# A graph attention layer: x_l rows of one tile in 22 pairs fetched one by one from SyncE, and the states cleared tile by tile

## Chip, cores and metric

The kernel runs on one core of a Trainium2 chip. The metric is the device time of one execution in microseconds. Before the change the median of 3 runs is 3961.25 us (3960.65 to 3964.16). The profile is of one further execution.

## The reference

A GATv2 layer with a feed-forward part, on 12,500 nodes with 128 features and 400,000 edges, sorted by their destination. `h` is the normalised and rectified input.

```python
x_l = (ln(h) @ W_l).reshape(n, H, C)          # H = 8 heads, C = 16
x_r = (ln(h) @ W_r).reshape(n, H, C)
e = (edge_attr @ W_e).reshape(-1, H, C)       # 32 attributes per edge, and a loop per node
m = leaky_relu(x_l[src] + x_r[dst] + e, 0.2)
alpha = einsum('ehc,hc->eh', m, att)
a = softmax of alpha over the edges of one destination
out = segment_sum(x_l[src] * a, dst) + bias
h = h + out
return x + h + gelu(ln(h) @ W1 + b1) @ W2 + b2
```

The costly part is `x_l[src]`: 400,000 rows in an order that only the data know.

## The kernel before

The nodes are 98 tiles of 128. First comes a **start** (`tile_gnn`): in rounds of 4 tiles, x is normalised, multiplied by W_l and written to `xl_dram` as rows of 136 words (544 bytes; 128 features and 8 ones). The x_l rows of a round are made by VectorE (L595) in one of three buffers and stored by SyncE (L603). In round 14 of the start SyncE loads the source indices of all edges (`src_sb`, L797). Meanwhile GpSimd gathers raw rows of x for 29 chosen pairs of units (L301), whose x_l rows are made later, so that these pairs need no gather of x_l.

Then comes the **edge loop** (`window_edges`). A unit is 256 edges, a pair is two units, so 512 edges in 4 tiles of 128; there are 782 pairs. The order of all engines is written out by hand (`manual_schedule`): round r runs the stages of different pairs, each with its lateness against the pair:

- `gather` (4 rounds ahead): GpSimd issues one indirect DMA (L980) per tile of 128 edges, four for a pair, into one of 12 buffers `xs`. Pairs of the 29 read their rows by one SyncE load (L975).
- `windows` (3 rounds ahead, every fourth pair): SyncE loads the edge attributes `ea` (L994), the destinations `dl` and `du` (L999, L1004), reads an address from `win_sb` into a register (L955) and loads the x_r rows `zw` (L1010).
- `place`: VectorE makes the selection matrices from `dl` (L1020) and `du` (L1027).
- `combine`: TensorE transposes the four tiles of `xs` into `z` (L1034) and adds x_r and e with one more matmul (L1037). It is the first to read the gathered rows.
- `apart`, `slope`, `bend`, `score`, `lowest`, `weigh` (L1043 to L1075): the leaky ReLU, the scores, their least value and the exponentials.
- `turn`, `keep_turned`, `collect` (L1083 to L1097): the weights are transposed, and `collect`, 6 rounds late, multiplies them with `xs` into `acc`. It is the last to read the gathered rows.
- `own_heads` (L1106, L1112) brings `acc` into a record `rec` of 16 destinations for each unit, and `put` (7 rounds late, L1122) writes both records from SyncE to `state_dram`, at an address read from `base_sb` every fourth pair. A put waits for the put before it, since the address is only known at run time.

State rows that no put writes must hold zeros and a large least score. `clear` (L745) writes those, for 7 tiles of nodes at a time and each of the two states apart: group 0 at the end of the start, then one group in every 8th round up to round 104. From round 197 on, groups of 4 node tiles whose edges are done are finished (`f_...`): their states are read back (L1173), merged, and run through the feed-forward part. In the first 196 rounds SyncE also loads all edge attributes for their mean (`ea_s`, L1129), every second round.

All loads and stores named here go through SyncE's queue in the order of the program; each waits for its semaphores there, and what follows waits behind it. In a round that order is: early steps of the finishing groups, the stages (of which SyncE has L975), `ea_s`, the clear, the finishing groups, the x_r and late x_l work, `windows`, `put`.

Of the kernel before, what the change touches and what calls it, by code (L numbers as in the profile page):

```python
# [13 lines left out]
F32 = mybir.dt.float32  # L14
BF16 = mybir.dt.bfloat16
I32 = mybir.dt.int32
U8 = mybir.dt.uint8
# [5 lines left out]
P = 128  # L23
# [19 lines left out]
OW = 172  # L43
OS = 176
PW = OR * OS
BEFORE = 12
AFTER = 3
WN = P - DE
# [14 lines left out]
BUSY = 5  # L63
LEAD = 2
KEPT = 7
BIG = 2.0**126
CAP = 2.0**120

# [76 lines left out]
def tile_gnn(  # L145
# [56 lines left out]
    src_sb = keep.tile([P, NCH * K], I32, name="src_sb")  # L202
    base_sb = keep.tile([1, NU // UP], I32, name="base_sb")
    win_sb = keep.tile([1, NU // QU], I32, name="win_sb")
    flag = keep.tile([1, 1], I32, name="flag")
    quads = [(t, min(GN, NT - t)) for t in range(0, NT, GN)]
    VAR = 6
# [532 lines left out]

    empty = keep.tile([P, H, SH], F32, name="empty")

    def clear(g):
        for st in state:
            nc.sync.dma_start(  # L745
                st.rearrange("(t p h) f -> p t (h f)", p=P, h=H)[:, g * GT : (g + 1) * GT, :],
                empty.rearrange("p h f -> p (h f)")[:, None, :].to_broadcast([P, GT, SW]),
            )

    node_stages = (  # L750
        (0, x_stats),
# [16 lines left out]
    with tc.manual_schedule():  # L768
        load_first()
        make_identity(nc, ident)  # L770
        for t in xls:
            nc.vector.memset(t[:, :, P:], 1.0)
        load_weights()
        load_x(0, min(GN, NT))
        load_raw()
        load_x(GN, min(3 * GN, NT - GN))
        for t in range(4 * GN, NT, 14):
            load_x(t, min(14, NT - t))
        load_dst()
        load_consts()  # L780
        nc.vector.memset(empty, 0.0)
        nc.vector.memset(empty[:, :, C + 1 : SH], CAP)
        rows_at = [i * 5 // 4 for i in range(len(raw))]
        for r in range(max(max(len(qs), 9) + LAST + 1, 16 + PARTS, rows_at[-1] + KEPT + 1)):
            if r == 0:
                count_up()
            for d, at in zip(raw, rows_at):
                if r == at:
                    raw_gather(d)
                if r == at + KEPT:  # L790
                    raw_store(d)
            if r == 3:
                weights()
            if r == 9:
                last_of_units()
            if r == 14:
                nc.sync.dma_start(src_sb, src)  # L797
# [24 lines left out]
        clear(0)  # L822
    pre.close()

    fast = nc.values_load(flag[0:1, 0:1], min_val=0, max_val=1)
    with tc.If(fast == 1) as cmp:
        window_edges(
            tc, n_edges, ea_t, NT, NE, NUE, ident, wer, weh, negrep, diag, nid, farw, bias_r, b2_r, w1_sb, w2_sb,
            cols, xl_dram, xl_t, xr_dram, xr_t, dc_dram, du_dram, late_dram, state_dram, state, clear, xr_steps, qs, raw_steps, raw, x_t, out_t, h_sb, src_sb, base_sb, win_sb, wid,
        )  # L830
    with cmp.Else():
        any_edges(
# [64 lines left out]

def window_edges(
    tc, n_edges, ea_t, NT, NE, NUE, ident, wer, weh, negrep, diag, nid, farw, bias_r, b2_r, w1_sb, w2_sb,
    cols, xl_dram, xl_t, xr_dram, xr_t, dc_dram, du_dram, late_dram, state_dram, state, clear, xr_steps, qs, raw_steps, raw, x_t, out_t, h_sb, src_sb, base_sb, win_sb, wid,  # L900
):


# [25 lines left out]
    with ExitStack() as es:  # L929
# [34 lines left out]
        def states_at(at):  # L964
# [4 lines left out]
                "u (n f) -> n u f", f=SH * 4  # L969
            )  # L970

        def gather(c):
            xs = rows.tile([P, KP, XW], F32, name="xs")
            if c in of_raw:
                nc.sync.dma_start(xs, late_dram[of_raw[c]["i"]])  # L975
                pairs[c]["xs"] = xs
                return
            for t in tiles_of(c):
                for j in t:
                    nc.gpsimd.indirect_dma_start(  # L980
                        out=xs[:, j, :],
                        out_offset=None,
                        in_=xl_dram,
                        in_offset=bass.IndirectOffsetOnAxis(ap=src_sb[:, c * KP + j : c * KP + j + 1], axis=0),
                    )
            pairs[c]["xs"] = xs
# [42 lines left out]
        def combine(c):  # L1029

            d, e = pairs[c], sum(edges_of(c))
            z = ps2.tile([P, EPR], F32, name="z")
            for j in range(e // P):
                nc.tensor.matmul(  # L1034
                    z[:, j * P : (j + 1) * P], d["xs"][:, j, 0:P], ident, start=(j == 0), stop=False, is_transpose=True
                )
            nc.tensor.matmul(z[:, :e], d["zw"], d["ea"][:, :e], start=False, stop=True)  # L1037
            d["z"] = z
# [51 lines left out]
        def collect(c):  # L1090
# [4 lines left out]
            for i, js in enumerate(tiles_of(c)):  # L1095
                for j in js:
                    nc.tensor.matmul(  # L1097
                        d["acc"][:, i, :], d["pt"][:, j * P : (j + 1) * P], d["xs"][:, j, :],
                        start=(j == js[0]), stop=(j == js[-1]),
                    )  # L1100

# [456 lines left out]
        CLEAR = 8  # L1558
# [379 lines left out]
```

## Time and profile before

| | |
|---|---|
| median of 3 runs | 3961.25 us |
| the profiled execution | 3956.45 us |
| its span | 3954.7 us |
| PE (TensorE) busy | 3447.8 us, 87% |
| POOL (GpSimd) busy | 2956.0 us, 75% |
| DVE (VectorE) busy | 2792.9 us, 71% |
| ACT (ScalarE) busy | 2168.7 us, 55% |
| TensorE clock granted, mean | 0.943 |

The span runs from the first to the last instruction that the profiler saw; the execution has 1.75 us around it. SP is SyncE; instructions that only issue DMAs, set registers or wait are not counted as busy, so SP has no busy time of its own, but its issues and waits can be listed. A group of instructions is shown as line, engine, operation and tiles, with its count, its busy time, the mean of one in ns, and the idle time of its engine just before it with what ended most of it. "issue" there is time in which the engine waited for nothing that the profile shows. Rows of the kind "min/median/max" give durations in ns. A row of a waits view gives the total, the count and the longest. In rows that cut the span into stretches, each engine's busy time is followed by the granted clock, the mean busy share of the 16 DMA engines and their GB/s.

### The profile page before, as it was taken

To read this page: it belongs to the slowest core of one execution; us is meant where nothing else is said; L and a number is where in the kernel's file an instruction comes from. 1 tells how busy PE (TensorE), PEld (TensorE's weight loads), DVE (VectorE), ACT (ScalarE), POOL (GpSimd) and SP (SyncE) were. 2 spreads that over 40 slices of the span, in tenths; PEclk is the share of its full clock that TensorE was granted. 3 is DMA by queue.
4 is the path that set the end of the run, shared out by engine and by line. 5 is a ranking of instruction groups with operands and counts; after the bars stand their busy time and mean duration, and the time that the engine had idled before them with its cause. 6 is when DMAs were issued, how large, how long until landed. Compare 5 with 4: busy or idle time off the path is not lost. (4 is left out here: it accounts for less than half of the span.)

```text
span 3954.7 us, 58500 instructions
## 1 busy us (share of the span) xinstructions
PE 3447.8 (87%) x18462; PEld 2358.8 (60%) x18463; DVE 2792.9 (71%) x6137; ACT 2168.7 (55%) x4747; POOL 2956.0 (75%) x3138
## 2 busy tenths in 40 slices
PE   4589898989898899999898898998889899889898
PEld 3356565656565666666665665666666566556565
DVE  6577777878776767677767776777767667667665
ACT  7445555655565555555555555555555555455444
POOL 7777777777777777777777777777777777777774
PEclk6799999999999999999999999999999999999999
DMA  8777787777666666666566666556556665655553
GB/s 225 214 183 190 195 201 194 184 176 168 164 128 124 128 122 123 128 123 120 115 122 128 124 123 128 123 119 125 117 124 125 127 122 108 122 119 114 122 118 74
DMA packets 579318, 552.09 MB, mean 140 GB/s; under 512 B 286689, under 2 KB 457282, under 8 KB 578578
## 3 DMA queue, kind: packets, MB, share of 16 engines
q1 hardware_dynamic: 478280, 330.80, 35.9%
q0 software_dynamic: 100000, 217.32, 28.5%
q8 instruction: 150, 2.46, 0.3%
q14 instruction: 168, 1.38, 0.1%
q10 hardware_dynamic: 720, 0.13, 0.0%
HBM read 482.05 MB, written 65.88 MB: 139 GB/s over the span
## 5 line engine op out<-in xcount | busy, mean ns | idle before, releaser
L980 POOL DMA_INDIRECT xs<-xl_dram,src_sb x3009 | 2841.7, 944 | 917.1 <-issue 798.0
L1075 ACT ACTIVATE p<-ab,rec 128x256 f32<-128x256 f32 x1563 | 655.2, 471 | 1025.8 <-DVE rec L1064 1021.3
L1106 DVE TENSOR_TENSOR own<-acc,diag 128x272 f32<-128x272 f32 x782 | 341.4, 437 | 811.5 <-PE acc L1097 809.5
L1097 PE MATMUL acc<-xs,pt 128*128 128x136 f32 x6250 | 891.6, 288 | 0.3 <-DVE own L1106 0.3
L1034 PE MATMUL z<-ident,xs 128*128 128x128 f32 x3125 | 552.9, 283 | 374.0 <-DMA xs<-xl_dram,src_sb 324.9
L1037 PE MATMUL z<-ea,zw 128*128 128x512 f32 x1564 | 852.7, 628 | 26.5 <-DVE ea L1020 11.3
L1034 PEld LDWEIGHTS z<-ident,xs 128*128 128x128 f32 x3125 | 398.4, 143 | 768.4 <-DMA xs<-xl_dram,src_sb 413.6
L1097 PEld LDWEIGHTS acc<-xs,pt 128*128 128x128 f32 x6250 | 820.7, 199 | 0.5 <-DVE own L1106 0.5
L1058 PE MATMUL ab<-m,negrep 128*128 128x512 f32 x1564 | 806.4, 597 | 0.0
L1088 ACT COPY pt<-pt_ps 128x512 f32<-128x512 f32 x782 | 454.9, 582 | 570.9 <-PE pt_ps L1083 568.9
L1053 DVE TENSOR_TENSOR m<-z,zs 128x512 f32<-128x512 f32 x782 | 532.8, 681 | 139.2 <-ACT zs L1048 138.1
L1083 PEld LDWEIGHTS pt_ps<-ident,p 128*128 128x128 f32 x3125 | 415.9, 148 | 360.1 <-issue 286.4
L1020 DVE TENSOR_SCALAR ea<-dl,wid 96x516 f32<-96x516 bf16 x782 | 575.8, 736 | 36.1 <-DMA dl<-dc_dram 36.1
L1064 DVE TENSOR_REDUCE rec<-ab 128x2 f32<-128x512 f32 x781 | 538.0, 689 | 13.1 <-PE ab L1058 12.5
L1083 PE MATMUL pt_ps<-ident,p 128*128 128x128 f32 x3125 | 499.4, 285 | 1.2 <-ACT xr L627 0.9
L1048 ACT ACTIVATE zs<-z 128x512 f32<-128x512 f32 x782 | 472.7, 604 | 41.7 <-DMA xs<-xl_dram,src_sb 34.9
L1112 DVE TENSOR_REDUCE rec<-own 128x34 f32<-128x272 f32 x782 | 340.8, 436 | 26.7
L1043 PE MATMUL ab<-ne,farw 128*128 128x512 bf16 x782 | 313.0, 400 | 28.4 <-ACT p L1075 25.7
L1037 PEld LDWEIGHTS z<-ea,zw 128*128 128x128 f32 x1564 | 256.5, 205 | 30.1 <-DVE ne L1027 10.3
L1058 PEld LDWEIGHTS ab<-m,negrep 128*128 128x128 f32 x1564 | 245.1, 194 | 1.1 <-DMA ea_s<-in_ea_t 0.7
L1043 PEld LDWEIGHTS <-farw 128*128 128x128 bf16 x782 | 79.5, 102 | 221.9 <-issue 110.2
L1075 ACT ACT_TABLE_LOAD x104 | 133.4, 1283 | 1.8
(237 smaller groups left out, 2167.4 us busy)
## 6 DMA issues: line engine op xcount, KB each, us to landing
dl<-dc_dram SPq DMA_DIRECT2D x196, 396.0 KB
ea<-in_ea_t SPq DMA_DIRECT2D x196, 256.0 KB
ea_s<-in_ea_t SPq DMA_DIRECT2D x98, 512.0 KB
xs<-xl_dram,src_sb POOLq DMA_INDIRECT x3009
state<-empty SPq DMA_DIRECT2D x28, 504.0 KB
state<-rec SPq DMA_DIRECT2D x781, 18.0 KB
f_st<-state SPq DMA_DIRECT2D x46, 288.0 KB
du<-du_dram SPq DMA_DIRECT2D x196, 64.0 KB
```

What stands on the lines that cost most here:

```text
L980: nc.gpsimd.indirect_dma_start(out=xs[:, j, :], out_offset=None, in_=xl_dram, in_offset=bass.IndirectOffsetOnAxis(ap=src_sb[:, c * KP + j ...
L1020: nc.vector.tensor_scalar(d["ea"][0:WN].rearrange("p (a b) -> p a b", b=OW), d["dl"][0:WN].rearrange("p (a b) -> p a b", b=OS)[:, :, 0:OW] ...
L1034: nc.tensor.matmul(z[:, j * P : (j + 1) * P], d["xs"][:, j, 0:P], ident, start=(j == 0), stop=False, is_transpose=True)
L1037: nc.tensor.matmul(z[:, :e], d["zw"], d["ea"][:, :e], start=False, stop=True)
L1048: nc.scalar.activation(d["zs"][:, :e], d["z"][:, :e], AF.Copy, scale=SLOPE)
L1053: nc.vector.tensor_tensor(d["m"][:, :e], d["z"][:, :e], d["zs"][:, :e], op=OP.max)
L1058: nc.tensor.matmul(d["ab"][:, :e], negrep.rearrange("p n h -> p (n h)"), d["m"][:, :e], start=False, stop=True)
L1064: nc.vector.tensor_reduce(d["rec"][:, :, CX], d["ab"].rearrange("p (u e) -> p u e", e=U), AX.X, OP.min)
L1075: nc.scalar.activation(d["p"][:, us], d["ab"][:, us], AF.Exp, bias=d["rec"][:, i, CX:SH], scale=-1.0)
L1083: nc.tensor.transpose(d["pt_ps"][:, js], d["p"][:, js], ident)
L1088: nc.scalar.copy(d["pt"][:, :e], d["pt_ps"][:, :e])
L1097: nc.tensor.matmul(d["acc"][:, i, :], d["pt"][:, j * P : (j + 1) * P], d["xs"][:, j, :], start=(j == js[0]), stop=(j == js[-1]),)
```

## The change

Of 35 pairs (31, 53, ... 779, none of the 29) GpSimd gathers only three tiles. The 128 rows of the fourth are fetched by SyncE, one DMA of 544 bytes each, into a tile of their own (`hand`, two buffers), spread over 22 rounds, 5 or 6 a round, at the start of the round. The last are issued 3 rounds before the pair's own. The byte addresses come from a small tile `hand_sb`, loaded in the start right behind `src_sb` as 35 x 128 single words and multiplied by 544 by VectorE two rounds later; SyncE reads 16 of them at a time into registers. Each row counts on one of 7 semaphores kept for this, and SyncE waits once for each tile for the full count, one round before the pair's. `combine` and `collect` read the fourth tile from `hand`.

`clear` now writes one tile of nodes in both states with one DMA: four of them at the end of the start, then one in every 4th round up to round 372, as the last thing of the round, behind the put.

```diff
+HAND_EVERY = 22
+HAND_FIRST = 31
+HAND_LEAD = 2
+HAND_READ = 16
+LANDED = 7
+CLEARED = 4
+CLEAR = 4
...
+def hand_pairs(nt, n_edges):
+    late = {c for c, _ in raw_pairs(nt, n_edges)}
+    hands = range(HAND_FIRST, n_edges // (UP * U), HAND_EVERY)
+    assert not late & set(hands)
+    return hands
...
-    def clear(g):
-        for st in state:
-            nc.sync.dma_start(
-                st.rearrange("(t p h) f -> p t (h f)", p=P, h=H)[:, g * GT : (g + 1) * GT, :],
-                empty.rearrange("p h f -> p (h f)")[:, None, :].to_broadcast([P, GT, SW]),
-            )
+    def clear(t):
+        both = state_dram[0 : UP * SR].rearrange("(a n) f -> a n f", a=UP)
+        nc.sync.dma_start(
+            both[:, (BEFORE + t * P) * H : (BEFORE + (t + 1) * P) * H].rearrange("a (p h) f -> p a (h f)", h=H),
+            empty.rearrange("p h f -> p (h f)")[:, None, :].to_broadcast([P, UP, SW]),
+        )
...
             if r == 14:
                 nc.sync.dma_start(src_sb, src)
+                nc.sync.dma_start(
+                    hand_sb,
+                    bass.AP(
+                        tensor=src.tensor, offset=src.offset + (hands[0] + 1) * UP * KU - 1,
+                        ap=[[hands.step * UP * KU, len(hands)], [NCH * K, P]],
+                    ),
+                )
+            if r == 16:
+                nc.vector.tensor_scalar(hand_sb, hand_sb, float(XW * 4), None, op0=OP.mult)
...
-        clear(0)
+        for t in range(CLEARED):
+            clear(t)
...
+        by_hand = {c: {"i": i} for i, c in enumerate(hands)}
+        landed = [tc.alloc_semaphore(f"landed{i}") for i in range(LANDED)]
+        def hand(r):
+            i, k = divmod(r + HAND_LEAD + hands.step - hands[0], hands.step)
+            if k == HAND_LEAD - 1 and 0 < i <= len(hands):
+                all_here = nc.sync.wait_ge(landed[(i - 1) % LANDED], ((i - 1) // LANDED + 1) * P * 16)
+                tc.declare_fence(all_here.ins, group=f"hand{i - 1}")
+            if not 0 <= i < len(hands):
+                return
+            d = by_hand[hands[i]]
+            if k == 0:
+                d["x"] = once.tile([P, XW], F32, name=f"hand{i % 2}")
+            for e in range(P * k // hands.step, P * (k + 1) // hands.step):
+                if e % HAND_READ == 0:
+                    d["at"] = words(hand_sb[i : i + 1, e : min(e + HAND_READ, P)], (NT * P - 1) * XW * 4)
+                row = nc.sync.dma_start(
+                    d["x"][e : e + 1, :].bitcast(U8), rows_at(xl_dram, d["at"][e % HAND_READ], 1, XW * 4)
+                )
+                row.then_inc(landed[i % LANDED], 16)
+                tc.no_tile_sem_insts.add(row.ins.name)
+                tc.add_to_no_dep_group(f"hand{i}", row.ins)
+        def row_of(c, j):
+            return by_hand[c]["x"] if c in by_hand and j == KP - 1 else pairs[c]["xs"][:, j, :]
...
                 for j in t:
+                    if c in by_hand and j == KP - 1:
+                        continue
                     nc.gpsimd.indirect_dma_start(
...
             for r in range(-AHEAD, max(last_round, groups[-1]["round"] + 18)):
                 in_round(r, early, groups[:-2])
+                hand(r)
...
-                if r > 0 and r % CLEAR == 0 and r // CLEAR < NT // GT:
-                    clear(r // CLEAR)
...
+                t, off = divmod(r, CLEAR)
+                if off == 0 and CLEARED <= t + CLEARED < NT and t >= 0:
+                    clear(t + CLEARED)
```

More of the change, by code (lines that the diff above doesn't have):

```diff
@@ L204, in tile_gnn @@
     win_sb = keep.tile([1, NU // QU], I32, name="win_sb")
+    hands = hand_pairs(NT, n_edges)
+    hand_sb = keep.tile([len(hands), P], I32, name="hand_sb")
     flag = keep.tile([1, 1], I32, name="flag")
@@ L828, in tile_gnn @@
             tc, n_edges, ea_t, NT, NE, NUE, ident, wer, weh, negrep, diag, nid, farw, bias_r, b2_r, w1_sb, w2_sb,
-            cols, xl_dram, xl_t, xr_dram, xr_t, dc_dram, du_dram, late_dram, state_dram, state, clear, xr_steps, qs, raw_steps, raw, x_t, out_t, h_sb, src_sb, base_sb, win_sb, wid,
+            cols, xl_dram, xl_t, xr_dram, xr_t, dc_dram, du_dram, late_dram, state_dram, state, clear, xr_steps, qs, raw_steps, raw, x_t, out_t, h_sb, src_sb, base_sb, win_sb, hand_sb, hands, wid,
         )
@@ L899, in window_edges @@
     tc, n_edges, ea_t, NT, NE, NUE, ident, wer, weh, negrep, diag, nid, farw, bias_r, b2_r, w1_sb, w2_sb,
-    cols, xl_dram, xl_t, xr_dram, xr_t, dc_dram, du_dram, late_dram, state_dram, state, clear, xr_steps, qs, raw_steps, raw, x_t, out_t, h_sb, src_sb, base_sb, win_sb, wid,
+    cols, xl_dram, xl_t, xr_dram, xr_t, dc_dram, du_dram, late_dram, state_dram, state, clear, xr_steps, qs, raw_steps, raw, x_t, out_t, h_sb, src_sb, base_sb, win_sb, hand_sb, hands, wid,
 ):
@@ L1034, in combine @@
                 nc.tensor.matmul(
-                    z[:, j * P : (j + 1) * P], d["xs"][:, j, 0:P], ident, start=(j == 0), stop=False, is_transpose=True
+                    z[:, j * P : (j + 1) * P], row_of(c, j)[:, 0:P], ident, start=(j == 0), stop=False, is_transpose=True
                 )
@@ L1097, in collect @@
                     nc.tensor.matmul(
-                        d["acc"][:, i, :], d["pt"][:, j * P : (j + 1) * P], d["xs"][:, j, :],
+                        d["acc"][:, i, :], d["pt"][:, j * P : (j + 1) * P], row_of(c, j),
                         start=(j == js[0]), stop=(j == js[-1]),
```

1 line of the change is left out of this document (removed).

## Prediction

> **What bounds the kernel now.** I read the page first, then the rows of the gather line, then the waits, then the chain of waits. Busy shares alone point to PE:
>
> ```profile
> span 3954.7 us, 58500 instructions
> PE 3447.8 (87%) x18462; PEld 2358.8 (60%) x18463; DVE 2792.9 (71%) x6137; ACT 2168.7 (55%) x4747; POOL 2956.0 (75%) x3138
> POOL 7777777777777777777777777777777777777774
> DMA  8777787777666666666566666556556665655553
> ```
>
> But POOL's digit never moves, although DMA falls from 8 to 5. The group and its waits say why:
>
> ```profile
> L980 POOL DMA_INDIRECT xs<-xl_dram,src_sb x3009 | 2841.7, 944 | 917.1 <-issue 798.0
> ...
> L980 POOL DMA_INDIRECT xs<-xl_dram,src_sb x3009: 940/944/1080, 151.6 to 3909.2; - x189
> ...
> POOL xs L980 <- issue: 798.0, 2618, 0.3
> PE z L1034 <- DMA xs<-xl_dram,src_sb: 324.9, 247, 4.1
> ```
>
> POOL spends 944 ns on a gather and 917.1/3009 = 305 ns before the next; no idle piece is over 0.3 us. From 151.6 to 3910.1 us that is 3009 x 1.249 = 3758 us, the whole stretch: POOL waits for nobody. PE does wait, 324.9 us in all, for gathers to land, so PE has some 8% of room. By stage, the pace is the same where the DMA engines are busiest (0.77) and where they are not (0.60):
>
> ```profile
> 200.00:1080.00 880.00, 773.39 (x4118) 525.24 (x4119) 670.11 (x1307) 473.13 (x1042) 665.14 (x705) 0.95 0.77 184
> 1980.00:3880.00 1900.00, 1703.56 (x9211) 1164.22 (x9210) 1318.73 (x2767) 1030.69 (x2109) 1436.62 (x1521) 0.96 0.60 121
> ```
>
> 665.14/880 and 1436.62/1900 are both 75.6% of POOL. The chain of waits at the end starts from the last gathers and needs about 45 us more, of PE, the last puts and the feed-forward:
>
> ```profile
> 3905.43 0.94 POOL xs L980
> ...
> 3907.92 3.38 DMA xs<-xl_dram,src_sb
> ```
>
> So the time is POOL's queue plus that tail. There are 782 pairs (29 of them fetched without POOL), so a round of the loop is 3758/782 = 4.805 us and 22 rounds are 105.7 us.
>
> **What the change removes.** `hand_pairs` gives 31, 53, ... 779: 35 pairs, each with one gather less. 35 x 1.249 = **-43.7 us** on the queue that sets the end, which leaves 104.5 us for 22 rounds. For PE nothing changes: the same 8 matmuls read `hand` in place of `xs`. PE's 8% of room covers a pace 1.2% quicker. The tail stays.
>
> **What it adds on SP.** 35 x 128 = 4480 one-row DMAs and 35 x 8 = 280 register loads of 16 words, spread over the 22 rounds before each use (about 6 rows a round). What SP has free decides. Its present load comes from its own waits:
>
> ```profile
> SPq L1122 <- DMA state<-rec: 352.9, 140, 8.2
> ...
> SPq L1122 <- DVE f_mn L1238: 0.2, 1, 0.2
> ```
>
> These are the first and the last of the 26 rows between 1980 and 2980 us; all 26 sum to 691.3 us, so SP works 308.7 of 1000 us, which is 32.6 us in 22 rounds. In 200 to 1080 us its 31 rows sum to 567.3 of 880, that is 37.6 us in 22 rounds; less the old clears (26 at 0.49 us), 36 us.
>
> No one-row DMA with a register address is in the trace. The nearest issues on SP are:
>
> ```profile
> L328 SPq DMA_DIRECT2D dc<-in_dst x1: 223/223/223, 27.9 to 27.9; - x1
> ...
> L337 SPq DMA_DIRECT2D dc<-in_dst x1: 272/272/272, 28.5 to 28.5; - x1
> ...
> L1010 SPq MOVE zw<-xr_dram x196: 29/35/42, 159.5 to 3897.5; - x196
> L1010 SPq DMA_DIRECT2D zw<-xr_dram x196: 332/343/359, 159.6 to 3897.6; - x196
> ...
> L955 SPq TENSOR_LOAD <-win_sb x196: 527/748/812, 158.7 to 3896.8; - x196
> L955 SPq TENSOR_LOAD <-base_sb x196: 299/307/331, 182.6 to 3926.9; - x196
> ```
>
> The first two fill one partition (257 and 4096 words) from fixed addresses. The third writes 96 partitions from a register address, after a move. Between two SP instructions lie some 0.045 us:
>
> ```profile
> 1510.11 0.41 SPq L994 DMA_DIRECT2D ea<-in_ea_t  x1
> 1510.57 0.42 SPq L999 DMA_DIRECT2D dl<-dc_dram  x1
> 1511.04 0.59 SPq L1004 DMA_DIRECT2D du<-du_dram  x1
> 1512.55 0.35 SPq L1010 DMA_DIRECT2D zw<-xr_dram  x1
> ```
>
> A row thus costs between 0.223 + 0.03 + 0.09 = 0.34 us and 0.343 + 0.035 + 0.09 = 0.47 us. I take **0.37**, from the middle of the two one-partition rows, whose shape it has. 128 x 0.37 = 47.4 us. A register load: 0.35 to 0.84 us with its gap; taken near the upper row, as it too follows DMA issues: 8 loads, 6 us.
>
> **The clears** move as well: 98 of 144 KB instead of 28 of 504 KB (14.1 MB both ways), one every 4 rounds up to round 376 rather than two every 8 up to 104, and now directly behind a put, on the same tensor. A clear has waited for a put before:
>
> ```profile
> SPq L745 <- DMA state<-rec: 19.6, 12, 2.2
> ...
> SPq L1122 <- DMA state<-empty: 85.8, 14, 9.3
> L745 SPq DMA_DIRECT2D state<-empty x28: 377/488/687, 153.4 to 665.0; - x28
> ```
>
> That is 1.63 us each with another issue in between; now next to nothing lies in between, so about 1.7 us of standing plus 0.45 of issue, 5.5 times in 22 rounds: 12 us of SP. The 85.8 us that puts stood behind clears shrink, but they are off POOL's path and earn nothing.
>
> From round 197 the finishing groups read the states back, and SP stands for landings that no row can fill:
>
> ```profile
> SPq L1122 <- DMA f_st<-state: 64.5, 24, 4.4
> SPq L1173 <- DMA state<-rec: 58.3, 25, 5.1
> ```
>
> 122.8 us over 585 rounds, 4.6 us in 22. SP in 22 rounds, against POOL's 104.5 us: rounds 7 to 196 (`ea_s` still loading) 36 + 47.4 + 6 + 12 = **101.4**; rounds 197 to 376 32.6 + 4.6 + 47.4 + 6 + 12 = **102.6**; later **90.6**. So SP just fits. Waits that stay, for the previous put's landing, are filled by the rows. I add 2.5 us for moments when SP is late: what stands behind it then are the window loads (L994 to L1010) that DVE's L1020 and PE's L1037 need two rounds on, and POOL feels that only after the 12 gather buffers are full, about 5 rounds (24 us) of lag.
>
> The new wait (one per hand tile) comes two rounds, 9.5 us, after the last row's issue, and a put lands within 2 us near the end:
>
> ```profile
> 3928.27 2.02 DMA state<-rec
> ```
>
> So it is normally past. Behind it in SP's queue stand the next rows, the windows and the put.
>
> On the DMA engines a row moves 544 bytes. The 72-byte packets of the puts took 7.8% of 16 engines in a 6.1 us stretch for 688 packets, 11 ns each, so even 16 pieces a row (71,680) are about 50 us per engine over 3,700: hidden.
>
> ```profile
> DMA packets 688, 0.05 MB, mean 8 GB/s; under 512 B 688, under 2 KB 688, under 8 KB 688
> ...
> q1 hardware_dynamic: 688, 0.05, 7.8%
> ```
>
> [...]
>
> **What it adds at the start.** The list of rows (`hand_sb`, 35 x 128 single words) is loaded behind `src_sb`, and DVE multiplies it two rounds later, in order:
>
> ```profile
> 71.97 0.70 SPq L797 DMA_DIRECT2D src_sb<-in_src  x1
> 76.74 1.09 DVE L595 SCALAR_TENSOR_TENSOR xl<-lr,roots_sb,bl_r 128x128 f32<-128x128 f32 x4
> ...
> 136.65 0.37 SPq L603 DMA_DIRECT2D xl_dram<-xl  x1
> ...
> 151.60 0.94 POOL L980 DMA_INDIRECT xs<-xl_dram,src_sb  x1 [0.30 <-issue]
> ```
>
> The load ahead of it:
>
> ```profile
> src_sb<-in_src SPq DMA_DIRECT2D x1, 1568.0 KB
> ...
> 72.00:74.00 2.00, 0.50 1.02 301
> ```
>
> DVE reaches the multiply at about 77.8 us. `src_sb`, 1568 KB at about 301 GB/s shared with the stores, is in by about 79. Single words were loaded before, 2 x 784 of them (L266):
>
> ```profile
> q1 hardware_dynamic: 794, 0.04, 168.2%
> ```
>
> 794 packets in the microsecond from 47 to 48, on 16 engines: 20 ns each per engine. [...] POOL loses 0 to 4 us; more if words come slower than those. I take **+4**, the upper end, as the stores queued behind the words land late too. [...] No row here shows a DMA of 35 rows.
>
> **The sum.** -43.7 + 4 + 2.5 = -37.2 us. The profiled execution took 3956.45 us (span 3954.7 and 1.75 around it): 3919.3. The median of the runs is 4.8 us above it, so **3924**; own range 3914 to 3941.
>
> **Rivals.**
> 1. **SP becomes the bound** (slower). With c the cost of a row, the first half fits only while some 54.6 + 128c stays under 104.5, c under 0.39 us. At `zw`'s 0.468 it needs 114.5 us: 8.8 us more than now in each of the 16.8 periods to round 376, +148, less 24 in the buffers; later 103, so the 18.4 periods of the second half still gain 22; with the start +4: +106, about **4067**. It is slower than before from c = 0.42 (16.8 x 2.5 = 24 + 22 - 4). For it: the wait sums, and that the row address sits in a register; against it: the one-partition issues. With also a dearer register load it goes beyond 4100.
> 2. **Marginal SP**: c near 0.41; the first half loses what the second gains: 3953 to 3969.
> [...]
> 4. **It does nothing**: PE takes over as the bound. Its 324.9 us of waiting for gathers speak against; time about 3960.
>
> **Chances.** Forecast 0.50, rival 1 0.26, rival 2 0.10, rival 3 0.11, rival 4 0.03 (rivals 2 and 4 make up "same"). A run tells about 0.2% (8 us) from no change. Faster 0.61, same 0.13, slower 0.26. Range 3908 to 4012: it takes in a row at 0.34 us (no stalls, no loss at the start: 3917), less 9 us for the spread between runs and what an overlap could add, and the lower half of rival 1; about 0.15 lies above it.
>
> **What would show it.** Right: 2974 gathers, still 944 ns with 305 between, the last one about 37 us earlier, PE's waits for gathers a little shorter, SP's row DMAs at 0.25 to 0.3 us. Wrong: POOL idle pieces of whole microseconds on the gather line (rival 1), window loads as releasers of DVE L1020; a first gather much later than 151.6 (rival 3).

## The result, and the profile after

The changed kernel takes a median of **4144.7 us** in 4 runs (4142.03 to 4151.94), against 3960.95 us (3958.65 to 3964.16) for the kernel before beside it: a ratio of 1.0466, 95% interval 1.0448 to 1.0484. It is 184 us slower, where 37 us less were forecast; the time lies above the range too (3908 to 4012). The line numbers from here on are those of the changed kernel: the gather is L1037, the place matrices L1077, `collect` L1154, the put L1179, the clear L762, the rows L1016, the register reads L982.

The page's head, and GpSimd's group on the page and in the rows of its line (shortest, median and longest in ns, first and last start):

```profile
span 4143.5 us, 67817 instructions
PE 3499.8 (84%) x18461; PEld 2394.4 (58%) x18463; DVE 2804.6 (68%) x6138; ACT 2161.9 (52%) x4747; POOL 2922.4 (71%) x3103
...
POOL 7776666656666667676667777777777777777774
...
L1037 POOL DMA_INDIRECT xs<-xl_dram,src_sb x2974 | 2808.1, 944 | 1135.4 <-issue 775.8
```

```profile
L1037 POOL DMA_INDIRECT xs<-xl_dram,src_sb x2974: 938/944/1073, 151.8 to 4094.0; - x199
```

The gathers are as forecast: 2974 of 944 ns, the first at 151.8 us (151.6 before). But POOL's digit, 7 in all 39 full slices before, is now 6 or 5 in many, up to about 2200 us, and idle time that is not "issue" has gone from 917.1 - 798.0 = 119 us to 1135.4 - 775.8 = 360 us. A view by stretch (busy time of PE, PEld, DVE, ACT and POOL, clock, DMA share, GB/s) says where:

```profile
300.00:1100.00 800.00, 635.51 (x3188) 433.41 (x3188) 525.53 (x1013) 364.79 (x806) 511.78 (x543) 0.88 0.66 151
1200.00:2150.00 950.00, 811.77 (x4294) 557.28 (x4294) 626.06 (x1323) 482.43 (x1003) 651.97 (x691) 0.92 0.59 123
2300.00:4000.00 1700.00, 1537.57 (x8374) 1050.22 (x8373) 1209.59 (x2536) 948.84 (x1944) 1285.24 (x1361) 0.97 0.62 123
```

The last stretch still has the old pace, 1285.24/1700 = 75.6% of POOL. The first has 64.0% and the second 68.6%. At 75.6% their 511.78 and 651.97 us of gathers would have taken 677 and 862 us: 123 and 88 us are lost there. The clears are issued from 153.6 to 2165.2 us; the loss ends with them.

What POOL waits for, and what stands behind that, among the waits of all engines (total, times, longest):

```profile
POOL xs L1037 <- issue: 775.8, 2543, 0.6
DVE ea L1077 <- DMA dl<-dc_dram: 332.2, 81, 9.4
POOL xs L1037 <- PE acc L1154: 256.2, 113, 9.0
PE z L1094 <- DMA zw<-xr_dram: 98.7, 28, 6.8
```

GpSimd stands 256.2 us for `acc`, so for gather buffers to come free; VectorE stands 332.2 us for `dl`, 36.1 before. `dl` comes from SyncE. One such place, SyncE's queue first, then VectorE and GpSimd in the same microseconds:

```profile
713.54 0.40 SPq L1179 DMA_DIRECT2D state<-rec  x1
718.24 0.39 SPq L762 DMA_DIRECT2D state<-empty  x1
718.73 1.93 SPq L1016 DMA_DIRECT2D hand<-xl_dram  x6
720.70 0.34 SPq L1051 DMA_DIRECT2D ea<-in_ea_t  x1
721.10 0.42 SPq L1056 DMA_DIRECT2D dl<-dc_dram  x1
```

```profile
726.22 0.75 DVE L1077 TENSOR_SCALAR ea<-dl,wid 96x516 f32<-96x516 bf16 x1 [6.44 <-DMA dl<-dc_dram]
...
731.41 0.94 POOL L1037 DMA_INDIRECT xs<-xl_dram,src_sb  x1 [2.88 <-PE acc L1154]
```

After the put's issue (713.54 to 713.94) SyncE stands 4.3 us until the put has landed and the clear may go; rows and windows wait behind. VectorE stands 6.44 us for `dl`, TensorE behind it, and GpSimd then finds no free buffer for 2.88 us. SyncE's own waits over the whole span, after and then before:

```profile
SPq L1179 <- DMA state<-rec: 269.1, 223, 4.2
SPq L762 <- DMA state<-rec: 256.5, 92, 5.3
SPq L1179 <- DVE rec L1169: 81.8, 92, 6.9
```

```profile
SPq L1122 <- DMA state<-rec: 1359.2, 547, 8.2
SPq L1122 <- DVE rec L1112: 739.1, 425, 8.9
```

Before, a put waited 739.1 us in all for its record: SyncE was ahead of the other engines and idle. After, that is 81.8 us, 63.4 of it after 2150 us: up to 1100 us SyncE hardly ever waits for work, as the next rows show (23.7 of 800 us, all that is not a put or a clear waiting for a landing). The stands of a put for the put before it have shrunk too, from 1359.2 to 269.1 us: most of that time is now filled with rows. The 256.5 us of clears standing for puts are new (21.2 before).

### The profile page after: what moved, and what is told of

Its sections match the earlier page's. It is cut to its first block, busy times and chain, and to the rows that moved or that the text cites. A ratio compares the mean times of both kernels' runs of the same rounds, so it can differ in the third digit from the quotient of the medians.

```text
span 4143.5 us, 67817 instructions
## 1 busy us (share of the span) xinstructions
PE 3499.8 (84%) x18461; PEld 2394.4 (58%) x18463; DVE 2804.6 (68%) x6138; ACT 2161.9 (52%) x4747; POOL 2922.4 (71%) x3103
## 3 DMA queue, kind: packets, MB, share of 16 engines
q0 software_dynamic: 98880, 214.89, 29.2%
## 4 chain that ended last, share of the span: by engine, by line
PE 38%; DMA 24%; DVE 10%; POOL 9%; issue 8%; SPq 8%; ACT 4%; POOLq 0%; DVEq 0%; ACTq 0%
POOL xs L1037 9%; PE acc L1154 9%; DMA xs<-xl_dram,src_sb 9%; PE z L1094 9%; PE ab L1115 7%; DMA state<-rec 5%; PE pt_ps L1140 5%; PE z L1091 4%; SPq L1016 3%; DMA dl<-dc_dram 2%; PE ab L1100 2%; DMA du<-du_dram 2%; DVE rec L1121 2%; SPq L982 2%; DMA zw<-xr_dram 1%
## 5 line engine op out<-in xcount | busy, mean ns | idle before, releaser
L1037 POOL DMA_INDIRECT xs<-xl_dram,src_sb x2974 | 2808.1, 944 | 1135.4 <-issue 775.8
L1094 PE MATMUL z<-ea,zw 128*128 128x512 f32 x1564 | 873.3, 642 | 187.2 <-DMA zw<-xr_dram 98.7
L1154 PE MATMUL acc<-xs,pt 128*128 128x136 f32 x6180 | 901.7, 292 | 4.1 <-DVE own L1163 3.5
L1154 PEld LDWEIGHTS acc<-xs,pt 128*128 128x128 f32 x6180 | 830.1, 203 | 5.2 <-DVE own L1163 4.1
L1115 PE MATMUL ab<-m,negrep 128*128 128x512 f32 x1564 | 816.0, 604 | 0.2 <-issue 0.2
L1077 DVE TENSOR_SCALAR ea<-dl,wid 96x516 f32<-96x516 bf16 x782 | 576.4, 737 | 332.3 <-DMA dl<-dc_dram 332.2
L1091 PE MATMUL z<-ident,xs 128*128 128x128 f32 x3090 | 523.7, 281 | 257.4 <-DMA xs<-xl_dram,src_sb 155.2
L1140 PE MATMUL pt_ps<-ident,p 128*128 128x128 f32 x3125 | 508.1, 289 | 8.3 <-ACT xr L644 4.6
L1105 ACT ACTIVATE zs<-z 128x512 f32<-128x512 f32 x782 | 473.5, 606 | 36.1 <-DMA state<-empty 28.3
L1100 PE MATMUL ab<-ne,farw 128*128 128x512 bf16 (+1 forms) x781 | 316.2, 405 | 44.9 <-ACT p L1132 41.6
L1192 DVE TENSOR_REDUCE part<-ea_s 128x1 f32<-128x1024 f32 x98 | 118.8, 1212 | 37.6 <-DMA ea_s<-in_ea_t 37.0
```

What stands on the lines that cost most here:

```text
L1037: nc.gpsimd.indirect_dma_start(out=xs[:, j, :], out_offset=None, in_=xl_dram, in_offset=bass.IndirectOffsetOnAxis(ap=src_sb[:, c * KP + j ...
L1077: nc.vector.tensor_scalar(d["ea"][0:WN].rearrange("p (a b) -> p a b", b=OW), d["dl"][0:WN].rearrange("p (a b) -> p a b", b=OS)[:, :, 0:OW] ...
L1091: nc.tensor.matmul(z[:, j * P : (j + 1) * P], row_of(c, j)[:, 0:P], ident, start=(j == 0), stop=False, is_transpose=True)
L1100: nc.tensor.matmul(d["ab"][:, :e], d["far"], d["ne"][:, :e], start=True, stop=False)
L1105: nc.scalar.activation(d["zs"][:, :e], d["z"][:, :e], AF.Copy, scale=SLOPE)
L1115: nc.tensor.matmul(d["ab"][:, :e], negrep.rearrange("p n h -> p (n h)"), d["m"][:, :e], start=False, stop=True)
```

## What SyncE's time was made of

The first and the last of 23 rows of SyncE's waits from 300 to 1100 us:

```profile
SPq L762 <- DMA state<-rec: 132.4, 36, 5.3
...
SPq L666 <- ACT zs L1105: 0.2, 1, 0.2
```

All 23 sum to 194.3 of 800 us; the other 605.7 are counted here as SyncE's work. A round has 2974/782 = 3.80 gathers, and 543 were made: 142.8 rounds of 5.60 us. In 22 rounds that is 93.3 us of work and 29.9 us of standing, 123.2 in all, where GpSimd needs 104.5. (The two parts fill the time by the way they are counted; that it is SyncE that holds the others up is seen in the 23.7 us above, all that it waits for other engines.) Of the standing, 20.4 are clears behind puts (3.7 us each), 5.9 puts behind the put before (38.2 us in the stretch), the rest small.

The durations of the parts that were forecast (rows, then reads):

```profile
L1016 SPq MOVE hand<-xl_dram x4480: 29/29/38, 182.6 to 4073.9; - x195
L1016 SPq DMA_DIRECT2D hand<-xl_dram x4480: 224/228/569, 182.7 to 4074.0; - x195
```

```profile
L982 SPq TENSOR_LOAD <-hand_sb x280: 980/1259/1514, 181.6 to 4065.4; - x140
L982 SPq TENSOR_LOAD <-win_sb x196: 510/802/951, 157.7 to 4078.4; - x196
L982 SPq TENSOR_LOAD <-base_sb x196: 302/558/718, 184.3 to 4114.4; - x196
```

Six rows take 1.91 to 1.93 us in the queue, 0.32 us apiece with the move and the gaps, below even the lower bound of the forecast. A read of 16 words takes 1.26 us, above its upper bound.

## The experiments

**Theory A**: SyncE's queue runs in order, and its issues and its stands for landings add up; where they pass 104.5 us in 22 rounds, the windows come late and GpSimd loses the difference. In its first form only the clears behind the puts (A1) cost, since each stands for the put's whole landing. **Rival B**: the rows themselves cost too much, in issues or in DMA traffic, with any clears. None of the kernels below leaves out part of the computation.

### e1_old_clears: the rows, with the old clears

Against the changed kernel (the bodies of `clear` as in the diff above):

```diff
-CLEARED = 4
-CLEAR = 4
+CLEAR = 8
...
-    def clear(t):
+    def clear(g):
...
-        for t in range(CLEARED):
-            clear(t)
+        clear(0)
...
+                if r > 0 and r % CLEAR == 0 and r // CLEAR < NT // GT:
+                    clear(r // CLEAR)
...
-                t, off = divmod(r, CLEAR)
-                if off == 0 and CLEARED <= t + CLEARED < NT and t >= 0:
-                    clear(t + CLEARED)
```

> The changed kernel, but with the clears as before (7 tiles of nodes at a time, each state apart, in the middle of every 8th round up to round 104). Theory A (the clears behind the put are what SyncE has no room for): SyncE's work in 22 rounds is 36 to 38 us as before, 128 rows at 0.318 us and 8 register loads at 1.3 us, about 88 to 90 us with some 9 us of other standing, under the 104.5 us that GpSimd needs; so GpSimd never waits, 2974 gathers x 1.249 us are 43.7 us less than before: 3915 to 3930 us. Theory B (the rows and register loads alone are too much for SyncE while it also loads ea_s): still slow in the first 1100 us, GpSimd at about 65 us busy in 100 there, 4030 to 4100 us.

Measured 4006.61 us beside 3961.7, ratio 1.0113 (1.0097 to 1.013). That is in neither of the two expected ranges. Of the loss, 4144.7 - 4006.6 = 138 us belong to the new clears; but the rows beside the old clears still lose 45 us against before, so 45 + 43.7 = 89 us against what was hoped. POOL's rows by stretch (the gather line alone, L1035 here), and SyncE's waits from 300 to 1100 us:

```profile
300.00:800.00 500.00, 321.24 (x341) 0.87 0.72 167
800.00:1100.00 300.00, 219.02 (x232) 0.95 0.76 168
...
2300.00:3800.00 1500.00, 1133.76 (x1202) 0.96 0.62 123
```

```profile
SPq L1177 <- DMA state<-empty: 66.1, 11, 6.7
SPq L1177 <- DMA state<-rec: 61.7, 53, 3.3
```

At 75.6%, 321.24 us of gathers take 425 us: 75 us are lost from 300 to 800 us, in the rounds with old clears (up to round 104) and just after; 10 us more to 1100; nothing late. There the puts stand for the clears, 6 us each. A1 falls: a clear need not stand behind a put to cost.

### e2_clears_only: the new clears without rows

Against the kernel before (the bodies of `clear` as in the diff above):

```diff
+CLEARED = 4
+CLEAR = 4
...
-    def clear(g):
+    def clear(t):
...
-                if r > 0 and r % CLEAR == 0 and r // CLEAR < NT // GT:
-                    clear(r // CLEAR)
...
+                t, off = divmod(r, CLEAR)
+                if off == 0 and CLEARED <= t + CLEARED < NT and t >= 0:
+                    clear(t + CLEARED)
```

> The kernel before with only the clears changed: one tile of both states in every 4th round, behind the put, nothing fetched by SyncE. Theory A: SyncE works about a third of the time there, so 2 to 4 us of standing in every 4th round are taken from its waiting: 3955 to 3968 us, GpSimd without a stall. Theory C (a put behind a clear behind a put is a serial chain that starves the window loads by itself): slower by a good part of the 184 us of the change, 4010 us or more.

Measured 3960.93 us beside 3961.7, ratio 1.0 (0.999 to 1.0009). SyncE stands just as long (300 to 1100 us; L747 is the clear):

```profile
SPq L1125 <- DMA state<-rec: 305.7, 123, 5.2
SPq L747 <- DMA state<-rec: 135.8, 43, 5.0
```

135.8 us for the clears, as in the changed kernel (132.4), but here puts wait another 305.7 us: SyncE has that room. The clears cost nothing by themselves, and 138 us beside the rows.

### e3_clears_mid: the new clears at the old place in the round

Against the changed kernel; the lines come to stand behind the `ea_s` load and ahead of the finishing groups:

```diff
+                t, off = divmod(r, CLEAR)
+                if off == 0 and CLEARED <= t + CLEARED < NT and t >= 0:
+                    clear(t + CLEARED)
...
-                t, off = divmod(r, CLEAR)
-                if off == 0 and CLEARED <= t + CLEARED < NT and t >= 0:
-                    clear(t + CLEARED)
```

> The changed kernel with the clear moved within its round: after the gather stages and the ea_s load, where the old clear stood, so that the round's 6 rows lie between the last put and the clear. Theory A, in the form that the standing behind a put just issued is the price: the rows (1.9 us) cover most of the 2.0 to 3.7 us of standing, 22 rounds need 95 to 102 us, 3920 to 3950 us. If it is the number of clears and their landing, wherever they stand: little changes, 4080 to 4150 us.

Measured 4144.46 us beside 3961.7, ratio 1.0459 (1.044 to 1.0479): as the changed kernel. The stand only changes hands (300 to 1100 us):

```profile
SPq L1179 <- DMA state<-empty: 132.8, 36, 4.8
```

The form of Theory A in which only the stand behind a put just issued counts had expected 3920 to 3950 us; 4080 to 4150, for clears that cost wherever they stand, is the range that was met. Now the put waits for the clear, 3.7 us each, as the clear did for the put. It is not the place behind the put, but that each of the two must have landed before the other may go.

### e4_every_16: more rows, old clears

Against e1:

```diff
-HAND_EVERY = 22
+HAND_EVERY = 16
```

> As the first kernel of this call (old clears), but a tile of every 16th pair fetched by hand: 47 tiles instead of 35. GpSimd needs 58.7 us less than before, 75.6 us in 16 rounds. SyncE needs about 51 us for rows and register loads and 27 us for the rest, 78 us, so by Theory A it is now SyncE that sets the pace all through: GpSimd stalls in the second half too, 3960 to 4060 us. If SyncE's room is larger than this count: 3900 to 3910 us.

Measured 4472.61 us beside 3961.7, ratio 1.1286 (1.1267 to 1.1305), with 47 gathers less, and over 400 us above the upper of the two expected ranges; 29 us of that are a late start (last section). GpSimd is slow even late, where no clear and no `ea_s` stands in the queue:

```profile
2300.00:3800.00 1500.00, 998.58 (x1059) 0.92 0.54 110
```

2962 gathers in 782 rounds are 3.79 a round, so this is 279.6 rounds of 5.37 us. SyncE's 48 waits there sum to 150.7 us; its work alone is 1349.3/279.6 = 4.83 us a round, against 4.73 that GpSimd needs. With this many rows the work alone passes the bound, as B has it, but by little: of the 0.64 us lost in a round, 0.54 is standing. That is where the expectation went wrong. It counted 78 us of work in 16 rounds, and 77.3 were measured; the 8.6 us of standing beside it were not in it.

### e5_late_hands, e7_late_every_20 and e8_rows_unread: rows only where the queue has room

e5 against e1 (rows from round 205 on); e7 has HAND_EVERY = 20 besides:

```diff
-HAND_FIRST = 31
+HAND_FIRST = 229
```

e8 against e5: all four tiles are gathered and read, the rows are fetched but not read:

```diff
-            return by_hand[c]["x"] if c in by_hand and j == KP - 1 else pairs[c]["xs"][:, j, :]
+            return pairs[c]["xs"][:, j, :]
-                    if c in by_hand and j == KP - 1:
-                        continue
```

> Old clears, and hand tiles only from pair 229 on (26 of them, rows from round 205), when neither clears nor ea_s loads are in SyncE's queue any more. Theory A2 (SyncE's queue, its work together with its standing for landings, is the price, and it is over GpSimd's pace only while clears stand among the puts): no GpSimd stall at all, 26 x 1.249 = 32.5 us less than before, 3927 to 3932 us. Theory D (rows one by one also cost elsewhere, on the DMA rings or on the gathers' landing): the gain is missing or smaller, 3945 us or more.

> As the first kernel of this call, a tile of every 20th pair (28 tiles). By the count of the second half (SyncE's work about 87 us in 22 rounds at every 22nd pair, some 11 of standing that nothing fills): 93 + 11 = 104 in 22 rounds, just at GpSimd's pace: 35 us less with no or few stalls, 3925 to 3940 us. If the limit lies higher up, near every 22nd: 3950 us or more, GpSimd stalling in the second half.

> As the first kernel of this call in what SyncE does, but GpSimd gathers all four tiles of every pair as before and the hand tiles are fetched and not read. Theory A2: GpSimd sets the pace and SyncE fits, so the rows are free and the time is that of the kernel before, 3956 to 3966 us; the difference to the first kernel is then all of it GpSimd's 26 gathers. Theory D: slower than before by what the rows cost, 3970 us or more.

Measured beside 3958.57 us: e5 3926.66, ratio 0.9921 (0.9907 to 0.9934); e7 3923.28, 0.9909 (0.9894 to 0.9925); e8 3958.75, 1.0001 (0.9992 to 1.001). e5 has 26 gathers less, 26 x 1.249 = 32.5 us, and gains 31.9; e7 has 28, 35.0, and gains 35.3; e8 removes none and issues the 3328 rows for 0.2 us. So a removed gather is worth its whole 1.249 us, and rows cost nothing while SyncE has room. (e5 and e7 come out 0.3 and 1.7 us below their expected ranges.) B's traffic is out. The gather line of e5, first where the old clears but no rows are in the queue, then where the rows go out and no clears; both are 75.6%:

```profile
300.00:1100.00 800.00, 604.66 (x641) 0.96 0.75 185
1200.00:2150.00 950.00, 718.28 (x761) 0.97 0.58 125
```

### e6_clears_first and e11_clears_first_20: clears over before the rows begin

e6 against e1: the old clears are done by round 39, the rows begin in round 51. e11 has HAND_EVERY = 20 besides.

```diff
-CLEAR = 8
+CLEAR = 3
...
-HAND_FIRST = 31
+HAND_FIRST = 75
```

> Old clears, but a group in every 3rd round so that all are done by round 39, and hand tiles from pair 75 on (33 of them, rows from round 51). Rows, register loads and ea_s loads share SyncE from round 51 to 196, without clears. Theory A2 by the count: 36 + 41 + 10 us of work and some 9 of standing in 22 rounds, 96 of 104.5: 33 x 1.249 = 41 us less, 3920 to 3930 us. If ea_s with the rows is too much by itself, as the 72.7 us of GpSimd in 100 between 800 and 1100 us of the kernel with old clears suggest: that stretch loses 4%, some 25 us, 3940 to 3955 us.

> The kernel of e9 once more, since in that call the kernel before itself took 4764 us. Old clears in every 3rd round (done by round 39), hand tiles of every 20th pair from pair 75 on, 36 tiles. By the count 45 us less than before, less some 5 us for the dense clears: 3914 to 3922 us. If every 20th pair is too much for SyncE beside the ea_s loads: GpSimd stalls between 400 and 1100 us, 3925 to 3945 us.

e6: 3922.54 us beside 3958.57, ratio 0.9914 (0.99 to 0.9927), the shortest of all: 33 gathers less are 41.2 us, and it gains 36.0. e11: 3981.96 us (3977.49 to 3986.17) beside 3959.92, ratio 1.0054 (1.0037 to 1.0071), above both expectations: with a row tile in every 20th pair instead of every 22nd the gain is gone. From 600 to 1100 us, `ea_s` still being loaded, the gather lines of e6 and of e11:

```profile
600.00:1100.00 500.00, 378.04 (x401) 0.96 0.72 173
```

```profile
600.00:1100.00 500.00, 357.30 (x380) 0.93 0.73 163
```

e6 holds the full 75.6%, e11 71.5%, a loss of 27 us there; from 1100 to 1400 us it makes 12 gathers less (229 against 241), 15 us. SyncE's waits from 600 to 1100 us sum to 63.1 us in e11; with 380 gathers, 3.80 a round, that is 96.2 us of work and 13.9 of standing in 22 rounds, where 92 and 9 to 11 had been counted. Rows at every 20th pair beside `ea_s` pass the bound, while later (e7) they fit. The two ran on different chips, so the size of the step is less sure than its direction.

### e12_tile_clears_first: the new clears, one in every round, over before the rows

Against the changed kernel; the clears are done by round 93, and 31 tiles are left:

```diff
-CLEAR = 4
+CLEAR = 1
...
-HAND_FIRST = 31
+HAND_FIRST = 119
```

> The kernel of e10 once more, for the same reason. Clears by tile behind the put in every round, done by round 93, hand tiles of every 22nd pair from pair 119 on, 31 tiles. If only the meeting of clears and rows in the same rounds counts: 38.7 us less than before, 3919 to 3930 us. If a clear behind every put costs by itself, where SyncE has no rows: 3935 us or more, with GpSimd stalls in the first 500 us.

Measured 4053.98 us (4051.7 to 4059.99) beside 3959.92, ratio 1.0242 (1.0224 to 1.0259). The first row, the gather line, and SyncE's queue:

```profile
L1016 SPq DMA_DIRECT2D hand<-xl_dram x3968: 224/228/544, 747.1 to 3983.6; - x199
```

```profile
300.00:400.00 100.00, 65.14 (x70) 0.84 0.69 162
400.00:500.00 100.00, 60.37 (x64) 0.84 0.67 158
500.00:580.00 80.00, 43.37 (x46) 0.87 0.62 146
```

```profile
503.18 0.39 SPq L1179 DMA_DIRECT2D state<-rec  x1
506.55 0.37 SPq L762 DMA_DIRECT2D state<-empty  x1
506.97 0.47 SPq L1186 DMA_DIRECT2D ea_s<-in_ea_t  x1
509.22 0.39 SPq L1179 DMA_DIRECT2D state<-rec  x1
```

No row is issued before 747.1 us, and GpSimd is down to 54 to 65% from 300 us on. From the put to the clear it is 3.4 us, from the clear to the next put 2.7: a round with both takes 6.0 us, against 4.8, though only three DMAs are issued in it. Over the six such rows from 300 to 800 us the loss adds up to 102 us, 83 of it before 700 us and so before any row. The start is 15 us late as well, for a reason of its own (last section).

### The runs beside a slower kernel before

e11 and e12 were first run as e9 and e10; then clears only, one in every round (e13: e2 with CLEAR = 1), e6 again (e14) and e11 again (e15); and these three once more (e16 to e18).

> Old clears in every 3rd round (done by round 39), hand tiles of every 20th pair from pair 75 on: 36 tiles, the most that the runs so far leave room for. By the count 36 x 1.249 = 45 us less than before, less some 5 us that the dense clears cost: 3915 to 3922 us. If rows of every 20th pair are too much beside the ea_s loads (36 + 56 of work and 9 to 11 of standing in 22 rounds, 101 to 103 of 104.5): stalls of GpSimd between 400 and 1100 us, 3925 to 3945 us.

> The changed kernel with its own clears by tile behind the put, but one in every round, so that all are done by round 93, and hand tiles of every 22nd pair from pair 119 on (31 tiles, rows from round 95). If what counts is only that clears and rows are not in SyncE's queue in the same rounds, clears by tile are as good as the old ones: 31 x 1.249 = 38.7 us less, 3919 to 3930 us. If a clear by tile in every round costs something by itself (every put behind a clear, every clear behind a put): SyncE is behind in the first 500 us and the time is 3935 us or more.

> Kernel before with the clears by tile behind the put, one in every round (done by round 93), and no rows at all. Theory (what SyncE issues and what it stands for landings add up, rows or not): a put then stands for the clear before it and the clear for the put, about 5 us a round beside 1.6 us of other work, above the 4.8 us of a round, so the 89 rounds of the clears lose about 1.3 us each less some 24 us of lag: 4030 to 4065 us, with gaps on GpSimd between 300 and 700 us. Rival (clears cost only where rows stand in the queue too): 3957 to 3964 us, as with one clear in every fourth round.

> The clears in every third round, rows from pair 75, a tile in every 22nd pair, a second time, beside the same with every 20th pair on one chip. Theory (at every 22nd pair SyncE stays just under GpSimd's pace): 3920 to 3927 us as the first time. Rival (the first result was that of another chip, on which landings are quicker): 3940 us or more.

> The same with a tile in every 20th pair, beside the run with every 22nd. Theory (SyncE just over the pace while it loads ea_s, to about 1080 us): 3970 to 3990 us, some 55 us above every 22nd pair. Rival (the chip): within 6 us of the run with every 22nd pair.

> The kernel before with the clears by tile behind the put, one in every round, without rows, once more, since the kernel before itself took 4775 us beside the last try. Theory (issues and stands add up on SyncE, rows or not): 4030 to 4065 us, with gaps on GpSimd between 300 and 700 us. Rival (clears cost only where rows stand in the queue too): 3957 to 3964 us. In the last call it stood 20 us above the kernel before, which supports neither fully.

> Clears in every third round, a tile in every 22nd pair from pair 75, once more. Theory (SyncE just under GpSimd's pace): 3920 to 3930 us. Rival (the first result came from a chip with quicker landings): 3940 us or more.

> The same with a tile in every 20th pair, on the same chip as the run with every 22nd. Theory (SyncE over the pace to about 1080 us): 3970 to 3990 us. Rival (the chip made the difference): within 6 us of the run with every 22nd pair.

Beside these runs the kernel before itself took 4764 us (e9, e10), 4775 (e13 to e15) and 4725 (e16 to e18), so their times stand beside each other only. Why it did is not known; e9 and e10 have the same chip number on record as e1 to e4, beside which it took 3961.7 us. Against it: e9 5093.34 us (1.0695), e10 5011.71 (1.0517); e13 4794.94 (1.0055), e14 4994.74 (1.0465), e15 5119.87 (1.0726); e16 4753.45 (1.0058), e17 4885.23 (1.0326), e18 5025.68 (1.063). Rows lose more there: e6's kernel, which gained 36 us, loses 160 to 220. SyncE's queue shows that they take longer to issue (e17; a long group of 6 and a short one of 5 rows):

```profile
2603.05 5.67 SPq L1014 DMA_DIRECT2D hand<-xl_dram  x6
...
2611.49 1.64 SPq L1014 DMA_DIRECT2D hand<-xl_dram  x5
```

The first is the longest of the five groups of six from 2600 to 2640 us, which take 1.86 to 5.67 us, 3.75 in the median; the nine of e1 from 700 to 760 us take 1.89 to 3.65, 1.92 in the median. Why is not settled. On one chip every 20th pair is 125 us (e15 against e14) and 140 us (e18 against e17) above every 22nd, which agrees in sign with e11 against e6. e13 and e16, clears in every round and no rows, are 20 and 28 us above the kernel before, in neither of the ranges expected at the ordinary speed. The page of e13 says why it is so little: its 3009 gathers and the idle time ahead of them are 2840.8 + 1698.1 us, over 782 rounds 5.8 us a round, not 4.8. With a round that slow, one of 6.0 us as in e12 loses only 0.2 us, over some 90 rounds 18 us (an estimate from these two rounds). The loss at the ordinary speed is seen in the first 747 us of e12, where no row is issued either.

### What follows

Theory A holds in its second form: **SyncE's issues and its stands for landings add up, wherever the clear stands in the round** (93.3 and 29.9 us in 22 rounds of the changed kernel, where GpSimd needs 104.5; with the clears behind the put 4144.7 us, in mid-round 4144.5). B's traffic is out (e8: 3958.75 us beside 3958.57), B's issues are part of A (e4). Not tried: a kernel in which puts and clears need not wait for each other's landing, which the run-time address forbids as written.

## Why the prediction was wrong

**Right.** GpSimd's queue bounds the kernel before, and a gather less is worth 1.249 us: e5 31.9 of 32.5, e7 35.3 of 35.0. Row bytes on the DMA engines are hidden (e8, with 3328 rows: 3958.75 us beside 3958.57). The wait for a tile's rows costs nothing in e5 and e7. The forecast of 3924 us lies near e6 (3922.5), which in this sense is the kernel that was priced, one whose clears are out of the way; that the two are so close is partly chance, since e6 removes 33 gathers and not 35, and gains 36.0 us of their 41.2. The signs that the prediction gave for rival 1 are those that came: idle pieces of whole microseconds on the gather line, and window loads as what VectorE waits for.

**The step that failed: "So SP just fits".** In 22 rounds, up to round 196:

| | forecast | measured, 300 to 1100 us |
|---|---|---|
| rows | 47.4 | 40.7 (128 x 0.318) |
| register reads | 6 | 10.9 (8 x 1.26 and gaps) |
| all work | 92 | 93.3 |
| clears standing for puts | 9.4 (5.5 x 1.7) | 20.4 |
| other standing | 0 | 9.5 |
| sum | 101.4 | 123.2 |

The work was right to 1.5 us, but by errors that nearly cancel: the rows were 6.7 us too dear, the reads 4.9 too cheap (they were priced by loads of 1 and 4 words), and what remains was 38.5 in place of 41.7. The standing was wrong twice.

First, "12" for the clears took 1.7 us of standing from rows in which the clear came in mid-round, well after the put. Directly behind the put it stands for nearly the whole landing, 3.7 us. e3 shows that moving it back would not have helped: the put then stands for the clear.

Second, "Waits that stay, for the previous put's landing, are filled by the rows". That holds for most of them (1359.2 us before, 269.1 after), but not for all. Rows fill only the time between a put's issue and the next wait; the rows of a round come in one burst of 1.9 us ahead of the other work, and behind a clear the put before it has to be waited for in full. No row is issued while the queue stands (none from 713.94 to 718.24 us, in the rows above). 9.5 us stayed, 5.9 of them puts behind puts.

Between 1200 and 2150 us the same holds: 47 rows of waits sum to 204.0 us, 691 gathers are 181.7 rounds of 5.23 us, 115 us in 22 rounds where 102.6 were forecast. After 2300 us GpSimd keeps its pace, as forecast.

**Rivals.** Rival 1, SP as the bound, is what happened, but not as it was priced: it hung on a row at 0.42 us or more, and rows cost 0.32. Its 4067 and the upper end of 4012 were too low since they varied the issues, never the standing: at 123.2 us, (123.2 - 105.7) x 8.6 periods to round 196 and (115 - 105.7) x 8 to round 372, 150 + 74, less 22 gained later and 24 in the buffers, give 178 beside the 184 measured. That is no second proof, since 123.2 and 115 are the pace of the changed kernel itself. (The last clear stands in round 372, not 376 as the prediction has it; no sum moves by more than 2 us.)

**The start.** 4 us were taken, and no run shows that term: the first gather comes at 151.8 us in place of 151.6, 0.2 us later, and 0.5 and 0.6 us later in e5 and e7, but 15.1 in e12 and 29.2 in e4 (last section). In the changed kernel VectorE stood 7.3 us for the row list, and the last x_l store went out at 140.75 us, 4.1 us later than before; GpSimd lost next to nothing by it. The sign given for rival 3, a first gather much later than 151.6 us, did not come here:

```profile
85.43 0.22 DVE L823 TENSOR_SCALAR hand_sb<-hand_sb 35x128 int32<-35x128 int32 x1 [7.34 <-DMA hand_sb<-in_src]
```

## What to carry to other kernels

A queue in program order has a budget of issues **and** stands (93.3 and 29.9 us in 22 rounds here): count each wait for a landing from the issue of what it waits for, less only the work that stands between the two in the queue. Work placed there filled the wait here (the puts' stands fell from 1359.2 to 269.1 us); work behind the waiting instruction did not, since nothing passed it (3.7 us for each clear behind its put). Waits that cost nothing today (739.1 us for records here) are the room that work moved to that queue uses up; when it was gone (23.7 of 800 us were left), the stands for landings turned into time (22 rounds took 123.2 us, where GpSimd needs 104.5). Two transfers that had to wait for each other's landing took about the sum of both (3.4 and 2.7 us, 6.0 a round, in e12), and which came first made no difference (3.7 us a stand in the changed kernel and in e3), so keep them out of rounds that are full.

## What the runs showed that was not expected

- **The stands for the row list do not go by its length.** VectorE stood 7.3 us for 35 x 128 single words, 7.1 for 26 (e5), 7.1 for 28 (e7), 6.0 for 33 (e6) and 8.8 for 36 x 128 (e11), but 28.1 us for 31 (e12) and 42.2 us for 47 (e4):

```profile
106.19 0.22 DVE L823 TENSOR_SCALAR hand_sb<-hand_sb 31x128 int32<-31x128 int32 x1 [28.15 <-DMA hand_sb<-in_src]
```

```profile
120.31 0.22 DVE L822 TENSOR_SCALAR hand_sb<-hand_sb 47x128 int32<-47x128 int32 x1 [42.22 <-DMA hand_sb<-in_src]
```

  The first gather then comes at 166.7 and 180.8 us instead of 151.6. Why the stands differ so is not shown. In e12, from 99 to 105 us, when hardly anything else moves (1 GB/s), the 16 DMA engines are busy under a tenth of the time, so under 1.6 of them on average. From 31 to 47 rows the stand grows by 14.1 us for 2048 words, 7 ns each.
- A DMA of one row from a register address issues in 228 ns on SyncE, a read of 16 words into registers in 1.26 us, one of 1 word in 0.80 us and one of 4 words in 0.56 us (`win_sb`, `base_sb`). Why one word takes longer than four stays open.
